# The set-up stage of a graph-attention kernel: row products three search pieces behind the copies they read, loads of W and x four pieces later

## The chip, the cores and the metric

The kernel runs on one core of a Trainium2 chip. The metric is device time in microseconds (us), of which less is better. The core has a tensor engine (TensorE, PE in the profile), a vector engine (VectorE, DVE), a scalar engine (ScalarE, ACT), GpSimd (POOL) and SyncE (SP), each with its own queue of instructions. ScalarE, SyncE and GpSimd also issue transfers (DMAs), which 16 DMA engines carry out.

## The reference

There are 4096 nodes with 128 features each, and a random 4096 x 4096 adjacency matrix of 0 and 1 in which a row has about 32 ones. Layer 0 is graph attention with 8 heads, layer 1 takes quantiles over a part of each node's neighbours. Cut to what matters:

```python
# layer 0
Wh = jnp.einsum('nd,hde->hne', nodes, W)
f1 = jnp.einsum('hnd,hd->hn', Wh, a1)
f2 = jnp.einsum('hnd,hd->hn', Wh, a2)
e = jax.nn.leaky_relu(f1[:, :, None] + f2[:, None, :], negative_slope=ALPHA)
att = jax.nn.softmax(jnp.where(mask, e, -9e15), axis=-1)
h = jax.nn.elu(jnp.einsum('hnm,hmd->hnd', att, Wh))
x = jax.nn.elu(cat @ W1 + b1)          # cat: the heads side by side
out = _layernorm(nodes + x, gamma, beta)
# layer 1: of each node's neighbours, without each skip-th, three quantiles
svals = jnp.sort(jnp.where(keep[:, :, None], x[None, :, :], big), axis=1)
agg = sum(w_q * picked(q) for q in (0.25, 0.5, 0.75))
agg = 0.5 * agg + 0.5 * x
out = agg @ W.T + b + x
```

The part that the change is in computes f1 and f2. The kernel does it as nodes times (W a1) and nodes times (W a2): 16 numbers for a node.

## The kernel before

The nodes are worked on in 32 tiles of 128, in three blocks of 4, 9 and 19 tiles. For a block the kernel first searches the adjacency rows for the neighbours' numbers (`neighbours`), then ranks the nodes by their number of neighbours, scatters one record for each node to DRAM, and then gathers the neighbours' feature rows from DRAM with indirect transfers and computes the attention. The search of the next block runs beside the attention of the one before. Layer 1 follows when all tiles are done: gathers, then sorting networks on VectorE.

The stage that matters here is the first: the search of the block of 4 tiles, with nothing to run beside it but the set-up. All of it stands ahead of the first gather. The order on TensorE, VectorE, ScalarE and GpSimd is fixed when the program is built, and in this stage it is the one in which the code names the instructions, except that at its end the small operations of the ranking stand among those that complete the records. An instruction that waits holds up whatever stands behind it on its engine. SyncE's queue is not ordered by the code in this way.

The search is a generator that stops after every piece. One piece (there are 43 for this block) handles 512 columns of one tile of 128 rows. TensorE makes a key for each column with two matmuls (L683, L686) from the signs of the adjacency row; there are two buffers for keys. VectorE takes the eight largest keys of each 128 columns (the "eights", four MAX8 at L650) one piece later. Beside that, for the tile before, it finds the next eight neighbours of the whole row (`best`: MAX8 at L655 and a replacement at L657). Pieces 0 to 31 make keys, pieces 8 to 39 find the best, and pieces 40 to 42 complete the records (L723 to L758). ScalarE turns an adjacency half-tile (128 x 2048, 1 MB) into signs (L644), once in four pieces and four pieces ahead of use; there are two buffers for signs. Right after each sign it issues the load of a later half-tile (L637); there are three buffers for those.

The set-up of the rows is a second generator, `node_rows` (L544), which is advanced by one step after every piece but the first (L326 to L328). It loads W (L550), a1, a2 (L554) and Wl (L556), then x in four quarters (L561), all from ScalarE's queue. VectorE multiplies W with a1 and a2 and sums (`wprod`, L567, L570), which gives `wa`. Then, for four tiles at a time, TensorE transposes x (L587), ScalarE copies the transposes to `xT` (L589), TensorE multiplies them with `wa` to `f_ps` (L581), and ScalarE copies that to `F` (L576). When all 32 tiles are done, VectorE clamps F into the records (L592) and SyncE stores x and f2 to `xt_d` (L594), from which the attention gathers. VectorE also computes a check on F (`sq` and `fm`, L604 to L609), and TensorE transposes Wl (L612).

After that VectorE, in `rank_by_count`, makes the ranks (L817 to L826), GpSimd scatters the records (L230), SyncE reads them back in the new order (L862, L888), and the first gather (L221) follows.

Of the kernel before, what the change touches and what calls it, by code (L numbers as in the profile page):

```python
# [9 lines left out]
F32 = mybir.dt.float32  # L10
# [9 lines left out]
P = 128  # L20
# [3 lines left out]
NT = N // P  # L24
# [220 lines left out]
def kernel(  # L245
# [61 lines left out]
    with tc.tile_pool(name="setup", bufs=1) as sp, tc.tile_pool(  # L307
# [15 lines left out]
        )  # L323
        iota(nc, rowi, [[1, P]])
        rows = node_rows(tc, sp, pp, rec, x, W, W_sb, a1, a2, Wl, wa, WlT, ident, bad, xt_d)
        for i, _ in enumerate(search(0, BLOCKS[0])):  # L326
            if i > 0:
# [216 lines left out]
def node_rows(tc, sp, pp, rec, x, W, W_sb, a1, a2, Wl, wa, WlT, ident, bad, xt_d):  # L544


    nc = tc.nc
    c = NT // 4
    load = nc.scalar.dma_start
    load(W_sb, W.rearrange("h d e -> d h e"))  # L550
    yield
    a_b = sp.tile([P, 2, H * D], F32, name="a_b")
    for i, a in enumerate((a1, a2)):
        load(a_b[:, i, :], a.rearrange("h d -> (h d)").partition_broadcast(P))  # L554
    wl_sb = sp.tile([P, D], F32, name="wl_sb")
    load(wl_sb, Wl)  # L556
    yield
    for i in range(4):
        for _ in range(3):
            yield  # L560
        load(  # L561
            rec[:, ts(i, c), R_X : R_X + D],
            x[ts(i, c * P), :].rearrange("(t p) d -> p t d", p=P),
        )
    for i in range(2):
        wprod = sp.tile([P, H, D], F32, name="wprod")
        nc.vector.tensor_tensor(  # L567
            wprod, W_sb, a_b[:, i, :].rearrange("p (h d) -> p h d", h=H), ALU.mult
        )
        nc.vector.tensor_reduce(wa[:, ts(i, H)], wprod, AX.X, ALU.add)  # L570
        yield
    F = sp.tile([P, NT, 2 * H], F32, name="F")
    xT = f_ps = None
    for t in range(0, NT + 8, 4):
        if f_ps is not None:
            nc.scalar.copy(F[:, t - 8 : t - 4, :], f_ps)  # L576
            f_ps = None
        if xT is not None:
            f_ps = pp.tile([P, 4, 2 * H], F32, name="f_ps")
            for u in range(4):  # L580
                nc.tensor.matmul(f_ps[:, u, :], lhsT=xT[:, ts(u, P)], rhs=wa, start=True, stop=True)  # L581
            xT = None
        yield
        if t < NT:
            xt_ps = pp.tile([P, 4 * P], F32, name="xt_ps")
            for u in range(4):
                nc.tensor.transpose(xt_ps[:, ts(u, P)], rec[:, t + u, R_X : R_X + D], ident)  # L587
            xT = sp.tile([P, 4 * P], F32, name="xT", bufs=2)
            nc.scalar.copy(xT, xt_ps)  # L589
        yield  # L590
    for dst, src in ((R_F1, F[:, :, 0:H]), (R_X + D, F[:, :, H:])):
        nc.vector.tensor_scalar(rec[:, :, dst : dst + H], src, FMAX, -FMAX, ALU.min, ALU.max)  # L592
    for i in range(4):
        nc.sync.dma_start(  # L594
            xt_d[ts(i, c * P), :].rearrange("(t p) w -> p t w", p=P),
            rec[:, ts(i, c), R_X:],
        )
    pad = sp.tile([P, XW], F32, name="pad")
    nc.gpsimd.memset(pad[:, 0:D], 0.0)
    nc.gpsimd.memset(pad[:, D:], PADF)  # L600
    nc.sync.dma_start(xt_d[N:, :], pad)
    yield
    sq = sp.tile([P, NT, 2 * H], F32, name="sq")
    nc.vector.tensor_tensor(sq, F, F, ALU.mult)  # L604
    fm = sp.tile([P, NT], F32, name="fm")
    nc.vector.tensor_reduce(fm, sq, AX.X, ALU.max)

    nc.vector.tensor_scalar(fm, fm, FMAX * FMAX, None, ALU.is_le)
    nc.vector.tensor_scalar(bad[:, 3, :], fm, -1.0, 1.0, ALU.mult, ALU.add)  # L609
    yield  # L610
    wl_ps = pp.tile([P, 4 * P], F32, name="xt_ps")[:, 0:D]
    nc.tensor.transpose(wl_ps, wl_sb, ident)  # L612
    nc.scalar.copy(WlT, wl_ps)
# [882 lines left out]
```

## Time and profile before

| | |
|---|---|
| median of three runs | 3682.77 us (3679.86 to 3687.81) |
| the profiled execution | 4612.32 us, of which its span is 4610.5 us |
| busy over the span: PE, DVE, ACT, POOL | 1260.0, 2754.3, 399.4, 2364.5 us |
| L826, the ranks are ready | at 94.81 us |
| L221, the first gather is issued | at 112.40 us |
| gathers for the attention (L221) | 1127, mean 967 ns |
| gathers for the quantiles (L221) | 1024, mean 1052 ns |

The profile is of one execution, which took about 930 us longer than the timed runs. Its page shows busy times of each engine, the clock that TensorE was granted in 40 equal slices of the span (115 us each), the costliest groups of instructions by line, and the transfers. A line of the timeline has the start in us, the duration in us, the engine, the line in the code, the operation, what it writes and reads, and in brackets how long the engine had been idle before and what ended that. A "q" behind an engine's name is its queue of transfer issues: the time given is that of the issue, not that of the transfer.

### The profile page before, as it was taken

Reading aid. Unit: us, or ns where it says so; the run is one execution under the profiler, and the core shown is the slowest. Engines: PE = TensorE matmul, PEld = TensorE weight load, DVE = VectorE, ACT = ScalarE, POOL = GpSimd, SP = SyncE. Lnnn points to the kernel's source line nnn. Section 1 sums busy time; section 2 is a strip of 40 time slices with the busy share of each in tenths; the row PEclk is TensorE's granted clock in tenths of the full one; section 3 lists DMA queues with packets and bytes.
Section 4 is the critical chain, followed back from the end, with each engine's and each line's share of the span. In section 5 each row is a group of like instructions: output and inputs, shape, how many; then the busy total and the mean of one; then the engine's idle time right before and its main releaser. Section 6 shows DMA issues by size and latency. Waiting matters only on the chain. (4 is left out here: it accounts for less than half of the span.)

```text
span 4610.5 us, 23017 instructions
## 1 busy us (share of the span) xinstructions
PE 1260.0 (27%) x5372; PEld 961.7 (21%) x5375; DVE 2754.3 (60%) x7608; ACT 399.4 (9%) x555; POOL 2364.5 (51%) x2344
## 2 busy tenths in 40 slices
PE   5264546555243425334245000000000000000001
PEld 2023323333243425324245000000000000000001
DVE  6274446655142212212254289989987977887788
ACT  2020212211011001000001000000000000000000
POOL 1616543243755566464532756677665355565530
PEclk9995556555556555555555555555555555555555
DMA  5321423220211111111110111111111011111100
GB/s 186 92 90 48 141 69 101 96 94 23 61 43 38 43 43 50 36 45 45 45 29 20 50 35 39 41 44 42 41 38 34 24 32 31 36 39 37 36 22 4
DMA packets 109537, 237.71 MB, mean 52 GB/s; under 512 B 47072, under 2 KB 63456, under 8 KB 101200
## 3 DMA queue, kind: packets, MB, share of 16 engines
q0 software_dynamic: 74464, 156.55, 12.2%
q10 hardware_dynamic: 14848, 70.85, 4.5%
q1 hardware_dynamic: 20080, 8.77, 0.8%
q8 instruction: 44, 0.72, 0.1%
q14 instruction: 101, 0.83, 0.1%
HBM read 224.85 MB, written 11.15 MB: 51 GB/s over the span
## 5 line engine op out<-in xcount | busy, mean ns | idle before, releaser
L221 POOL DMA_INDIRECT G<-xt_d,idx x1127 | 1090.3, 967 | 1109.5 <-PE y L1012 696.0
L221 POOL DMA_INDIRECT vals<-x_d,idx x1024 | 1076.9, 1052 | 337.5 <-issue 302.0
L1223 DVE TENSOR_TENSOR work<-work 128x512 f32<-128x512 f32 (+6 forms) x1405 | 960.6, 712 | 35.8 <-remote 22.1
L1223 DVE TENSOR_TENSOR work<-work,work 128x512 f32<-128x512 f32 (+5 forms) x958 | 605.6, 656 | 47.6 <-remote 35.7
L1242 PE MATMUL st_ps<-dg,goal 128*128 128x128 f32 x286 | 71.8, 430 | 1935.4 <-DVE goal L1223 1791.8
L1012 PE MATMUL y<-wide,G 128*128 128x32 f32 (+2 forms) x2254 | 463.1, 381 | 97.3 <-issue 71.6
L1242 PEld LDWEIGHTS st_ps<-dg,goal 128*128 128x128 f32 x286 | 63.9, 325 | 1941.5 <-issue 1940.6
L1012 PEld LDWEIGHTS y<-wide,G 128*128 128x128 f32 x2254 | 443.6, 297 | 120.4 <-issue 86.1
L976 DVE TENSOR_SCALAR rden<-small 4x256 f32<-4x256 f32 x32 | 13.0, 407 | 648.1 <-remote 583.6
L650 DVE MAX8 first<-key 128x8 f32<-128x128 f32 x1024 | 225.5, 282 | 253.6 <-remote 128.7
L230 POOL DMA_INDIRECT out_dram<-o,own_i x32 | 50.8, 1588 | 556.6 <-ACT o L1268 539.2
L1194 DVE COPY junk<-still 128x1 f32<-128x1 f32 x1295 | 194.6, 150 | 206.2 <-remote 97.4
L683 PE MATMUL key<-sgn,markb 128*128 128x512 bf16 x256 | 147.2, 575 | 398.9 <-DVE first L650 171.2
L982 PE MATMUL rz<-rden,ownT 4*128 4x32 f32 (+6 forms) x460 | 113.3, 416 | 515.9 <-DVE rden L977 431.4
L982 PEld LDWEIGHTS rz<-rden,ownT 4*128 4x128 f32 x460 | 101.8, 317 | 532.2 <-issue 364.0
L1031 PE MATMUL hT<-late,W_sb 128*128 128x128 f32 x512 | 112.8, 409 | 238.1 <-issue 160.2
L644 ACT ACTIVATE sgn<-adj_t 128x2048 bf16<-128x2048 int32 x64 | 122.1, 1908 | 557.3 <-PE key L683 273.5
L1223 DVE TENSOR_TENSOR work<-vals 128x1024 f32<-128x1024 f32 (+8 forms) x140 | 138.7, 1007 | 32.7 <-DMA vals<-x_d,idx 32.4
L1031 PEld LDWEIGHTS hT<-late,W_sb 128*128 128x128 f32 x512 | 104.7, 312 | 249.7 <-issue 167.1
L1241 ACT ACTIVATE dg<-ident,wt 128x128 f32<-128x128 f32 x143 | 47.6, 394 | 1191.8 <-PE st_ps L1242 1191.5
L686 PE MATMUL key<-parts,oneb 64*128 64x512 bf16 x256 | 146.5, 572 | 4.8 <-issue 4.6
L1042 PE MATMUL small<-W_sb,late 128*128 128x128 f32 x512 | 120.3, 429 | 33.4 <-DVE late L1039 33.4
(184 smaller groups left out, 1743.0 us busy)
## 6 DMA issues: line engine op xcount, KB each, us to landing
adj_t<-in_adj_dram ACTq DMA_DIRECT2D x64, 1024.0 KB
G<-xt_d,idx POOLq DMA_INDIRECT x1127
vals<-x_d,idx POOLq DMA_INDIRECT x1024
R<-rec_d SPq DMA_DIRECT2D x128, 26.2 KB
xt_d<-rec SPq DMA_DIRECT2D x4, 544.0 KB
rec<-in_x_dram ACTq DMA_DIRECT2D x4, 512.0 KB
narrow<-rec_d SPq DMA_DIRECT2D x72, 5.2 KB
a_b<-in_L_gnn_a_dram ACTq DMA_DIRECT2D x2, 512.0 KB
```

What stands on the lines that cost most here:

```text
L221: nc.gpsimd.indirect_dma_start(out=dst, out_offset=None, in_=rows, in_offset=bass.IndirectOffsetOnAxis(ap=idx, axis=0),)
L644: nc.scalar.activation(sgn, adj_t, AF.Sign, accum_out=cnt[:, i : i + 1])
L650: nc.vector.max(first[:, ts(c0 // CW + c, 8)], key[:, ts(c, CW)])
L683: nc.tensor.matmul(key, lhsT=markb, rhs=sgn[:, ts(b, 512)], start=True, stop=False)
L686: nc.tensor.matmul(key, lhsT=oneb[0:64, :], rhs=parts[1][:, ts(r - 1, 512)] if r else parts[0], start=False, stop=True)
L982: nc.tensor.matmul(rz[:, layer[i] * H : (layer[i] + w - g0) * H], lhsT=ownT[w][:, r, :], rhs=rden.rearrange("p (g r h) -> p r g h", r=k // ...
L1012: nc.tensor.matmul(yf[:, ts(g, c)], lhsT=G[:, col + j - a, 0:D], rhs=pf[:, ts(j, c)], start=(i == 0 and g % (w // 2) == w // 2 - 1), stop= ...
L1031: nc.tensor.matmul(hT[:, ts(h, P)], lhsT=consts["W_sb"][:, h, :], rhs=yT[:, h, :], start=True, stop=True)
L1042: nc.tensor.matmul(o, lhsT=hv[:, h, :], rhs=consts["W1_sb"][:, h, :], start=(h == 0), stop=(h == H - 1))
L1194: nc.vector.tensor_copy(junk, late["still"])
L1223: nc.vector.tensor_tensor(slots_of(dst, (j, c, s, m), size), slots_of(a, (i, c, s, m), size), slots_of(b, (i + d, c, s, m), size), op,)
L1242: nc.tensor.matmul(st_ps[:, u, :], lhsT=goal[:, (j * k + u) * D : (j * k + u + 1) * D], rhs=dg, start=(j == 0), stop=False,)
```

## The change

The change leaves every operation as it is and moves steps of `node_rows` to other places in the row of pieces. One more buffer for `xT` (three in place of two) is the only addition.

- The load of W moves from the first step to the fifth, those of a1, a2 and Wl from the second to the seventh. The four quarters of x are then two pieces apart and not three, so the first comes four pieces later, the last one piece later. The multiplication to `wa` and the transposes come one piece later.
- The product of four tiles with `wa` was made one piece after their transposes and their copy; it is now made three pieces after. The copy to F was made two pieces after the product and still is.
- The clamps, the stores to `xt_d`, the check on F and the transpose of Wl come three pieces later: they now stand among the pieces that complete the records.

```diff
@@ -547,8 +547,11 @@
     nc = tc.nc
     c = NT // 4
     load = nc.scalar.dma_start
+    for _ in range(4):
+        yield
     load(W_sb, W.rearrange("h d e -> d h e"))
-    yield
+    for _ in range(2):
+        yield
     a_b = sp.tile([P, 2, H * D], F32, name="a_b")
     for i, a in enumerate((a1, a2)):
         load(a_b[:, i, :], a.rearrange("h d -> (h d)").partition_broadcast(P))
@@ -556,7 +559,7 @@
     load(wl_sb, Wl)
     yield
     for i in range(4):
-        for _ in range(3):
+        for _ in range(2):
             yield
         load(
             rec[:, ts(i, c), R_X : R_X + D],
@@ -570,23 +573,24 @@
         nc.vector.tensor_reduce(wa[:, ts(i, H)], wprod, AX.X, ALU.add)
         yield
     F = sp.tile([P, NT, 2 * H], F32, name="F")
-    xT = f_ps = None
-    for t in range(0, NT + 8, 4):
-        if f_ps is not None:
-            nc.scalar.copy(F[:, t - 8 : t - 4, :], f_ps)
-            f_ps = None
-        if xT is not None:
+    turned, made = [], []
+    for t in range(0, NT + 12, 4):
+        if t >= 12:
+            nc.scalar.copy(F[:, t - 12 : t - 8, :], made.pop(0))
+        if 8 <= t < NT + 8:
             f_ps = pp.tile([P, 4, 2 * H], F32, name="f_ps")
+            xT = turned.pop(0)
             for u in range(4):
                 nc.tensor.matmul(f_ps[:, u, :], lhsT=xT[:, ts(u, P)], rhs=wa, start=True, stop=True)
-            xT = None
+            made.append(f_ps)
         yield
         if t < NT:
             xt_ps = pp.tile([P, 4 * P], F32, name="xt_ps")
             for u in range(4):
                 nc.tensor.transpose(xt_ps[:, ts(u, P)], rec[:, t + u, R_X : R_X + D], ident)
-            xT = sp.tile([P, 4 * P], F32, name="xT", bufs=2)
+            xT = sp.tile([P, 4 * P], F32, name="xT", bufs=3)
             nc.scalar.copy(xT, xt_ps)
+            turned.append(xT)
         yield
     for dst, src in ((R_F1, F[:, :, 0:H]), (R_X + D, F[:, :, H:])):
         nc.vector.tensor_scalar(rec[:, :, dst : dst + H], src, FMAX, -FMAX, ALU.min, ALU.max)
```

## The prediction

> **What bounds the kernel now.** I read the page's span and slices first, then the two stages' busy times, then the timeline from the first instruction to the first gather, and last the order in which the two built programs put their instructions on each engine.
>
> ```profile
> span 4610.5 us, 23017 instructions
> PEclk9995556555556555555555555555555555555555
> ```
>
> The change touches only what runs before the first gather, one of the forty slices. The reader is to see that it can win or lose microseconds, not per cent. The handover to the rest is this (start, duration, engine, line, operation):
>
> ```profile
> 94.81 0.17 DVE L826 CAST ranks<-rank 128x4 int32<-128x4 f32 x1
> 95.86 1.12 POOL L230 DMA_INDIRECT rec_d<-rec,ranks  x1 [54.61 <-issue]
> ...
> 112.40 0.97 POOL L221 DMA_INDIRECT G<-xt_d,idx  x1 [4.98 <-issue]
> ```
>
> VectorE computes the ranks, GpSimd scatters the records 1 us later, SyncE reads them back, GpSimd gathers. So this stage ends when VectorE reaches L826, and VectorE's idle time before it is what can be won. Busy time by stage (PE, PEld, DVE, ACT, POOL, clock, DMA share, GB/s):
>
> ```profile
> 20.00:40.00 20.00, 11.23 (x20) 1.94 (x19) 15.48 (x59) 8.01 (x8) 0.00 (x0) 1.00 1.05 358
> 40.00:60.00 20.00, 17.52 (x57) 9.80 (x57) 15.99 (x65) 6.49 (x11) 0.83 (x3) 1.00 0.35 117
> 60.00:80.00 20.00, 19.27 (x70) 12.86 (x70) 14.82 (x61) 6.80 (x13) 0.00 (x0) 1.00 0.40 126
> ```
>
> From 20 to 40 us the DMA engines are full; from 40 to 80 us TensorE is. VectorE has two kinds of gap. The first:
>
> ```profile
> 16.60 0.33 ACTq L637 DMA_DIRECT2D adj_t<-in_adj_dram  x1
> 17.61 0.39 ACTq L550 DMA_DIRECT2D W_sb<-in_L_gnn_W_dram  x1
> 18.03 2.34 ACTq L554 DMA_DIRECT2D a_b<-in_L_gnn_a_dram  x2
> 20.41 0.54 ACTq L556 DMA_DIRECT2D wl_sb<-in_L_gnn_W_dram  x1
> 21.00 1.91 ACT L644 ACTIVATE sgn<-adj_t 128x2048 bf16<-128x2048 int32 x1 [9.77 <-DMA adj_t<-in_adj_dram]
> 23.05 0.58 PE L683 MATMUL key<-sgn,markb 128*128 128x512 bf16 x1 [5.10 <-ACT sgn L644]
> 24.21 0.89 DVE L650 MAX8 first<-key 128x8 f32<-128x128 f32 x4 [4.34 <-PE key L686]
> ```
>
> ScalarE's queue issues W, a1, a2 and Wl ahead of the third sign, and the sign starts right after the last issue. Its bracket blames a transfer, but the issues before it fill the time up to 20.95. Key 8 then comes late and VectorE loses 4.34 us. The second kind:
>
> ```profile
> 48.34 1.12 PE L587 MATMUL xt_ps<-ident,rec 128*128 128x128 f32 x4
> 49.26 0.63 PE L683 MATMUL key<-sgn,markb 128*128 128x512 bf16 x1
> 50.36 1.89 PE L581 MATMUL f_ps<-wa,xT 128*128 128x16 f32 x8
> 52.08 0.59 PE L683 MATMUL key<-sgn,markb 128*128 128x512 bf16 x1
> ```
>
> The next transposes start at 53.14, so two pieces cost TensorE 4.80 us: transposes 0.92, key 1.10, products 1.72, key 1.06. It does not wait: the products start exactly 0.54 after the key's second half, and the copy xT had ended at 50.08. VectorE needs only 3.2 for two pieces. Its gaps in 43 to 75 us, from the same timeline, are 0.41, 0.36, 1.14, 0.62, 0.90, 0.29, 1.07, 0.32, 1.10, 0.36, 1.14, 0.62: together 8.33 us.
>
> **What the Trainium skill says.** "TensorE: Matmul & The Clock Gate", section "Back-to-back issue gap", gives N/1.2 ns for a cold matmul, 427 ns for 512 columns, and "LDWEIGHTS" adds P/1.2, 107 ns: 0.53 us. The trace has 0.54, although its clock row reads 1.00 here. "What's actually happening" has the warm clock at twice that; no run here shows it yet. The same page, "Architectural detail", calls ACT and DVE strict FIFO: the sign held behind the issues agrees. "DMA: Bandwidth & Descriptors", "Issuing engines are not separate DMA queues", says that all queues share the same 16 DMA engines; the share of 1.05 agrees, so landing times must be counted over all queues. "Perfetto Trace Analysis", the part on HWDGE DMA instructions, warns that data movement lies outside a DMA instruction's window; so I estimate landings from bytes.
>
> **Part 1, loads later.** No instruction is added or removed. In the new program ScalarE's order is: adjacency load (16.60, as before), third sign, next adjacency load, and only then W, a1, a2, Wl. The third adjacency tile was asked for by 2.15 us. Up to 12 us 3.7 MB had moved (sum of two-us windows: 37, 255, 402, 423, 413, 337 GB/s), more than the three tiles and W1 together (3.67 MB), so it should be there. The sign starts at 16.98 and not at 21.00: 4.02 us earlier, and key 8 and VectorE with it (24.21 to 20.19; it is free at 19.86, so 0.33 us of gap stays). Bound from the other side: a2's issue at 18.9 waits for that tile's semaphore, so the tile is there by then at the latest, and the gain is at least 2.1. I take 4.0.
>
> What now stands behind: the fourth sign, behind an adjacency issue (0.33), W 0.39, a1 and a2 2.34 and Wl 0.54, starts at 22.75. Key 12 needs it 2.05 later, at 24.8; it would otherwise come at 28.49 - 4.02 = 24.47. VectorE is a full microsecond behind TensorE there, so 0.3 is hidden; every microsecond of slower issue beyond that would show.
>
> W and a1 are needed by wprod, now after piece 16: 20.19 plus seven pieces (9.5 us to the eights of key 14, 1.15 for that piece, 0.35, 1.8) gives 33.0. Landing, estimated: 5.6 MB had moved by 19.4; six adjacency tiles, W1, the vectors, fills, W, a1 and a2 are 8.9 MB; the rest, 3.3 MB at 360 GB/s (20 to 34 us), takes 9 us: 28.4. Slack 4.6 us. The first x quarter comes 1.6 MB later, 33, and is needed at 41.2. Both hidden; if the cover were gone, the whole lateness would be VectorE's.
>
> **Part 2, products later.** Before, the transposes follow pieces 18, 20, ... 32 and the products pieces 19, 21, ... 33. After, the transposes follow 19, 21, ... 33 and the products 22, 24, ... 36. The last key is number 31. So between key 18 and key 31 TensorE had seven transposes and six products; it now has six and five. The lag removes no wait, as TensorE had none; it moves work behind the last key, where TensorE is idle.
>
> In time: VectorE sets the pace up to key 18, its eights move from 44.78 to 40.76. Pieces 19 to 21 hold two transposes and no products, so VectorE goes on at 1.6 a piece; key 22 ends at 46.4. From there TensorE is the bound again: products 1.72, key to 49.2, then four periods of 4.79. Key 31 starts at 48.1 + 19.2 = 67.3, before at 73.22. Its eights come 1.2 later, at 68.5 against 74.42: 5.95 us earlier. So part 2 gives 5.95 - 4.02 = 1.9 of the 8.33; the rest stays.
>
> **Part 3, the tail.** VectorE has the same 77 instruction rows from these eights to L826, only the two clamps and the four operations on sq stand later. The clamps need F: after key 31 TensorE does transposes, products, transposes, two products (7.0 us, to 75.3), the last copy ends at 76.4. The clamps stand at 74.42 to 86.77 less 2.15 of moved operations, 10.2 after the eights: 78.7. Slack 2.3 us. SyncE's four stores of xt_d then start at 79.2, 2.2 earlier than before (81.41). Their 2.23 MB took 8 us and overlap an adjacency load by about a microsecond, so they land near 88 to 89, ahead of the first scatter (95.86 - 5.95 = 89.9), and the gather that needs them is at 106.4. Nothing is added on POOL. Behind this, the engines' orders are the same; the first gather waits also for TensorE's and ScalarE's use of the third xT buffer, which is over 30 us before.
>
> **Sum.** 4.0 + 1.9 = 5.9 us. The profiled execution, 4612.3 us with 1.8 outside its span, would take 4606.4. The runs' median, 3682.8, is 25% shorter than the profiled execution; the stage is early and I find no reason to scale, so 3676.9. A measurement of this kernel can tell about 0.2%, 7.4 us, from no change.
>
> **Rivals.**
> (B) All of VectorE's gaps go, 4.0 + 8.3: 3670.4. For it: the gaps are all named as waits for keys. Against: two pieces' TensorE work sums to the period, so waits for copies are not what fills it. 0.14.
> (C) In the runs without a profile TensorE is warm, halving its 4.8 us below VectorE's 3.2; the second kind of gap is not there to win, and 4.0 or less is left: 3678.8. For it: the runs are 25% shorter. Against: 0.54 a key all along in the trace. 0.18.
> (D) W and a1 land late. VectorE stands at wprod; the forecast is used up when they land after 33.0 + 5.9 = 38.9. Before, the DMA engines empty only at 43.6; if W landed then, the wait is 10.6 and the time 3682.8 - 5.9 + 10.6 = 3687.5. For it: full DMA engines, one more adjacency tile ahead. Against: the 4.6 us of slack. 0.08.
> (A) The forecast: 0.60.
>
> **How the numbers follow.** A spans 3674 to 3680 by the bounds of part 1 and the issue times. To hold 8 in 10 the range takes in C, most of B and a few us of run-to-run spread (the three runs lie 8 us apart): 3669 to 3684. Faster by over 0.2%: nearly all of B and 0.17 of A's 0.60 by spread, 0.30. Slower by over 0.2%: most of D and a little spread, 0.08. The rest, 0.62, is within.
>
> **What would show it.** Right: third sign near 17, before the W issue; no 4.3 us gap at piece 8; eights of key 31 near 68.5; L826 near 88.9; first gather near 106.4; period still 4.8 us in the middle. Wrong: a VectorE gap ahead of L570 (D), periods under 4 us (B), or a first gather moved by 6 us and a total that does not follow.

## The result, and the profile after

The changed kernel took 3683.1 us (median of 12 runs, 3667.4 to 3691.6). The kernel before, run beside it, took 3687.2 us (12 runs, 3679.9 to 3696.0). The ratio is 0.9983 with a 95% interval of 0.9969 to 0.9997: 6.3 us less, and between 1.1 and 11.4 (it is not the ratio of the two medians, which lie 4.1 us apart). That is on the edge of what a measurement of this kernel can tell, and within the 0.2% that the prediction called no change.

The page of the changed kernel begins with its span and, further down, the clock that TensorE was granted in 40 slices of the span:

```profile
span 3688.3 us, 23015 instructions
...
PEclk9975665565575555555555555555555555555555
```

The two profiled executions differ by 922 us, which is no effect of the change: the profile of before and all of the later experiments are of executions with longer waits behind the set-up, in which either kernel takes some 4550 to 4600 us (medians). The set-up stage can be compared all the same, because in it the same operations last as long in both: a half of a key (one of its two matmuls) has a pitch of 0.54 us in either, and the changed kernel reaches the ranks within 0.22 us of the profile shown here in two such longer executions. So what follows reads that stage alone.

Busy time by stage of the changed kernel (window, then PE, PEld, DVE, ACT, POOL in us, clock, DMA share, GB/s):

```profile
20.00:40.00 20.00, 11.72 (x21) 2.05 (x21) 19.07 (x70) 6.01 (x6) 0.83 (x3) 1.00 1.05 354
40.00:60.00 20.00, 19.44 (x62) 10.78 (x63) 16.22 (x73) 6.36 (x10) 0.00 (x0) 1.00 0.53 172
60.00:80.00 20.00, 15.86 (x63) 11.73 (x62) 16.15 (x74) 7.08 (x15) 0.00 (x0) 1.00 0.32 103
```

VectorE works 19.07 us of the first window, before 15.48. In all three it works 51.44 us, before 46.29. The difference, 5.15 us, is about how much earlier the stage's work is done. TensorE is busy to the last from 40 to 60 us, as it was before from 60 to 80: the same work stands earlier.

The timeline of the changed kernel (start, duration, engine, line, operation; the line numbers behind L550 are two to four higher than before):

```profile
16.90 0.33 ACTq L641 DMA_DIRECT2D adj_t<-in_adj_dram  x1
17.34 1.91 ACT L648 ACTIVATE sgn<-adj_t 128x2048 bf16<-128x2048 int32 x1 [6.20 <-PE key L690]
19.37 0.33 ACTq L641 DMA_DIRECT2D adj_t<-in_adj_dram  x1
19.73 0.46 ACTq L552 DMA_DIRECT2D W_sb<-in_L_gnn_W_dram  x1
20.22 1.41 ACTq L557 DMA_DIRECT2D a_b<-in_L_gnn_a_dram  x2
20.55 0.89 DVE L654 MAX8 first<-key 128x8 f32<-128x128 f32 x4 [0.69 <-PE key L690]
21.66 1.95 ACTq L559 DMA_DIRECT2D wl_sb<-in_L_gnn_W_dram  x1
23.66 1.91 ACT L648 ACTIVATE sgn<-adj_t 128x2048 bf16<-128x2048 int32 x1 [4.32 <-PE key L690]
...
33.17 1.22 DVE L570 TENSOR_TENSOR wprod<-W_sb,a_b 128x1024 f32<-128x1024 f32 x1
...
49.59 1.12 PE L590 MATMUL xt_ps<-ident,rec 128*128 128x128 f32 x4
50.50 0.63 PE L687 MATMUL key<-sgn,markb 128*128 128x512 bf16 x1
...
51.60 1.89 PE L584 MATMUL f_ps<-wa,xT 128*128 128x16 f32 x8
...
54.49 0.89 DVE L654 MAX8 first<-key 128x8 f32<-128x128 f32 x4 [1.06 <-PE key L690]
...
68.87 0.89 DVE L654 MAX8 first<-key 128x8 f32<-128x128 f32 x4 [1.39 <-PE key L690]
...
75.91 0.20 ACT L579 COPY F<-f_ps 128x64 f32<-128x64 f32 x1
...
79.31 0.49 DVE L596 TENSOR_SCALAR rec<-F 128x256 f32<-128x256 f32 x2
...
89.41 0.17 DVE L830 CAST ranks<-rank 128x4 int32<-128x4 f32 x1
90.45 1.12 POOL L230 DMA_INDIRECT rec_d<-rec,ranks  x1 [51.17 <-issue]
...
107.30 0.97 POOL L221 DMA_INDIRECT G<-xt_d,idx  x1 [5.15 <-issue]
```

Read from the top: the third sign follows its adjacency issue at 17.34, and W, a1, a2 and Wl are issued behind it. Key 8's eights wait 0.69 us where they waited 4.34. `wprod` has no bracket: W and a1 were there. In the middle the two pieces' pattern of TensorE is as before, with transposes every 4.79 us (49.59, then 54.38), and VectorE's brackets are again about 0.3 and 1.1. The eights of key 31 stand at 68.87. In the profile of before they stood here:

```profile
74.42 0.90 DVE L650 MAX8 first<-key 128x8 f32<-128x128 f32 x4 [0.62 <-PE key L686]
```

The last copy to F ends 3.2 us before the clamps, the ranks come 5.40 us earlier (94.81 to 89.41) and the first gather 5.10 (112.40 to 107.30).

### The profile page after: what moved, and what is told of

Read it like the earlier page. It is cut to its first block, busy times and chain, and to the rows that moved or that the text cites. A ratio compares the mean times of both kernels' runs of the same rounds, so it can differ in the third digit from the quotient of the medians.

```text
span 3688.3 us, 23015 instructions
## 1 busy us (share of the span) xinstructions
PE 1235.0 (33%) x5375; PEld 940.7 (26%) x5375; DVE 2743.8 (74%) x7608; ACT 397.5 (11%) x555; POOL 2365.6 (64%) x2344
## 5 line engine op out<-in xcount | busy, mean ns | idle before, releaser
L221 POOL DMA_INDIRECT G<-xt_d,idx x1127 | 1121.8, 995 | 500.7 <-issue 324.8
L221 POOL DMA_INDIRECT vals<-x_d,idx x1024 | 1052.4, 1028 | 336.4 <-issue 298.1
L1016 PE MATMUL y<-wide,G 128*128 128x32 f32 (+2 forms) x2254 | 447.5, 376 | 27.2 <-DVE wide L1003 27.2
L1016 PEld LDWEIGHTS y<-wide,G 128*128 128x128 f32 x2254 | 427.0, 289 | 51.6 <-DVE wide L1003 30.2
L955 DVE TENSOR_TENSOR z<-G,f1x 128x128 f32<-128x128 f32 (+5 forms) x93 | 29.4, 328 | 430.8 <-DMA G<-xt_d,idx 429.5
L970 PE MATMUL small<-z,own 128*4 128x32 f32 (+6 forms) x460 | 50.1, 274 | 343.8 <-ACT z L962 343.8
```

What stands on the lines that cost most here:

```text
L221: nc.gpsimd.indirect_dma_start(out=dst, out_offset=None, in_=rows, in_offset=bass.IndirectOffsetOnAxis(ap=idx, axis=0),)
L1016: nc.tensor.matmul(yf[:, ts(g, c)], lhsT=G[:, col + j - a, 0:D], rhs=pf[:, ts(j, c)], start=(i == 0 and g % (w // 2) == w // 2 - 1), stop= ...
```

## The experiments

The theory: the two parts act one after the other on VectorE's chain, the loads with some 4 us and the lag of the products with some 2, and what the ranks gain goes whole into the time. The main rivals: only one of the parts does anything; or a gain so early is lost later. The first four kernels ran together, the next four together, the last two together.

| | third sign | wait at key 8 | eights of key 31 | ranks | key 8's eights to ranks | first gather | ratio to before, 95% interval |
|---|---|---|---|---|---|---|---|
| before, its profile | 21.00 | 4.34 | 74.42 | 94.81 | 70.60 | 112.40 | |
| before_again | 19.99 | 3.35 | 73.41 | 93.79 | 70.59 | 112.08 | 0.9989, 0.9963 to 1.0016 |
| loads_only | 17.28 | 0.64 | 70.59 | 91.10 | 70.60 | 108.64 | 0.9957, 0.9929 to 0.9985 |
| lag_only | 20.70 | 4.05 | 72.64 | 93.16 | 69.25 | 111.16 | 1.0003, 0.9975 to 1.0031 |
| delay40 | 17.86 | 1.23 | 69.39 | 130.07 | 108.99 | 147.90 | 1.0071, 1.0042 to 1.0099 |
| after, its profile | 17.34 | 0.69 | 68.87 | 89.41 | 68.86 | 107.30 | 0.9983, 0.9969 to 0.9997 |
| after_again | 17.07 | 0.43 | 68.63 | 89.19 | 68.90 | 107.04 | 0.9962, 0.9941 to 0.9983 |
| after_third | 17.09 | 0.45 | 68.63 | 89.19 | 68.88 | 107.24 | 1.0011, 0.9974 to 1.0048 |
| w_after_x | 17.27 | 0.61 | 75.13 | 95.68 | 75.20 | 113.53 | one run, 4596.6 us |
| late6 | 17.86 | 1.21 | 64.59 | 85.76 | 64.69 | 103.56 | 0.9977, 0.9944 to 1.0010 |
| late6_again | 17.27 | 0.62 | 65.08 | 86.25 | 65.77 | 104.01 | 1.0007, 0.9981 to 1.0032 |
| late7 | 16.70 | none | 61.82 | 84.76 | 64.85 | 104.52 | 0.9989, 0.9963 to 1.0015 |

All times are microseconds. The sixth column counts from the start of key 8's eights: what happens ahead of key 8, where the issues hold up the third sign, drops out of it. The kernel before took 4559.8, 4597.4 and 4558.2 us in the three groups. Its repeat in the same group came out at 0.9989, 5 us away from itself and with 12 us of interval to each side, so the total cannot part effects of 2 and 4 us here; the milestones in the traces can.

### before_again: the kernel before, unchanged

> The kernel before, unchanged, beside itself. It shows how far two equal kernels lie apart, and where the first gather stands in a second execution. Theory (the set-up stage alone decides): ratio 1.000 within 0.0015, ranks ready (L826) at 94.8 us, first gather at 112.4, two pieces of TensorE's dense part in 4.8 us. Rival (TensorE runs at twice the clock in undisturbed runs, so the second kind of gap isn't there): a key matmul to the next in 0.27 us and not 0.54, and the ranks earlier than 90.

In its timeline the same issues stand ahead of the third sign:

```profile
17.38 0.39 ACTq L550 DMA_DIRECT2D W_sb<-in_L_gnn_W_dram  x1
17.80 1.62 ACTq L554 DMA_DIRECT2D a_b<-in_L_gnn_a_dram  x2
...
19.46 0.48 ACTq L556 DMA_DIRECT2D wl_sb<-in_L_gnn_W_dram  x1
19.99 1.91 ACT L644 ACTIVATE sgn<-adj_t 128x2048 bf16<-128x2048 int32 x1 [8.95 <-issue]
...
23.20 0.89 DVE L650 MAX8 first<-key 128x8 f32<-128x128 f32 x4 [3.35 <-PE key L686]
```

The issues of a1 and a2 took 1.62 us, in the first profile 2.34, the issue of Wl 0.48 instead of 0.54, and the sign came 1.01 us earlier. The bracket now reads "issue", where the first profile named the adjacency transfer. So the sign waited for the issues ahead of it on ScalarE's queue, not for its data. It also gives the spread of one kernel's set-up: 1.0 us in the ranks, 0.3 at the first gather, where the fourth scatter happened to wait longer. All of that 1.0 us arises ahead of key 8: from its eights to the ranks it is 70.59 us here and 70.60 in the first profile.

### loads_only: the loads later, the products where they were

```diff
-    turned, made = [], []
-    for t in range(0, NT + 12, 4):
+    xT = f_ps = None
+    for t in range(0, NT + 8, 4):
...
-            xT = sp.tile([P, 4 * P], F32, name="xT", bufs=3)
+            xT = sp.tile([P, 4 * P], F32, name="xT", bufs=2)
```

(the loop of the kernel before, the loads of the changed one)

> The loads of W, a1, a2, Wl and x as in the changed kernel, the products one piece behind their transposes as before. Theory: the third sign starts near 17.3, the 4.3 us gap shrinks to 0.7, so 3.7 us come from here; TensorE then has six products between key 18 and key 31 and not five: eights of key 31 near 70.4 (before 74.4, changed 68.9), ranks ready near 91.0 (before 94.8, changed 89.4), ratio 0.9990. Rival (the gain is one of both parts together, or of the lag alone): ranks no earlier than 93.

```profile
70.59 0.89 DVE L653 MAX8 first<-key 128x8 f32<-128x128 f32 x4 [1.39 <-PE key L689]
...
91.10 0.17 DVE L829 CAST ranks<-rank 128x4 int32<-128x4 f32 x1
...
108.64 0.98 POOL L221 DMA_INDIRECT G<-xt_d,idx  x1 [4.99 <-issue]
```

The ranks come 3.71 us earlier than in the profile of before, 2.69 earlier than in before_again. Key 8 comes earlier by the same 3.71, and from there to the ranks it is 70.60 us as before. This is the larger part of the change, and it acts without the other. The total came out 20 us (7 to 32) below the kernel before, where 0.9990, some 5 us, was expected; nothing in the set-up accounts for the rest.

### lag_only: the products later, the loads where they were

```diff
-    for _ in range(4):
-        yield
     load(W_sb, W.rearrange("h d e -> d h e"))
-    for _ in range(2):
-        yield
+    yield
...
-        for _ in range(2):
+        for _ in range(3):
             yield
```

> The products three pieces behind, the loads as before. Theory: the 4.3 us gap stays; five products and not six between the keys 18 and 31: eights of key 31 near 73.0, ranks ready near 93.4, ratio 0.9996. Rival (TensorE's products did wait for ScalarE's copies, and the lag takes all of these waits away): VectorE's gaps between 43 and 75 us go from 8.3 to under 3, ranks before 89.

```profile
65.84 0.89 DVE L651 MAX8 first<-key 128x8 f32<-128x128 f32 x4 [1.11 <-PE key L687]
67.85 0.89 DVE L651 MAX8 first<-key 128x8 f32<-128x128 f32 x4 [0.36 <-PE key L687]
70.63 0.89 DVE L651 MAX8 first<-key 128x8 f32<-128x128 f32 x4 [1.14 <-PE key L687]
72.64 0.89 DVE L651 MAX8 first<-key 128x8 f32<-128x128 f32 x4 [0.62 <-PE key L687]
...
93.16 0.17 DVE L827 CAST ranks<-rank 128x4 int32<-128x4 f32 x1
```

The ranks come 1.65 us earlier than in the profile of before. The wait at key 8 is still 4.05, and VectorE's last eight brackets before key 31 (0.91, 0.29, 1.07, 0.33, 1.11, 0.36, 1.14, 0.62) are those that the prediction lists for before, to 0.01 us. If the lag had removed a wait of TensorE's, its periods would be shorter and these brackets smaller. There are only fewer of them, ten and not twelve: one transpose group and one product group have gone behind the last key.

The parts seem to add up, 3.71 + 1.65 = 5.36 against 5.40 together, but so close a sum is in part luck. Of the 1.65, 0.30 comes from key 8, which was earlier here because the row of issues ahead of the third sign happened to start earlier (17.31 against 17.61). Counted from key 8, the lag gives 1.35 us alone (69.25 against 70.60) and 1.74 beside the early loads (68.86 against 70.60 in loads_only). The parts add up to within 0.4 us; where these 0.4 come from was not looked into.

### delay40: the changed kernel with 32 multiplications on VectorE before the ranks

```diff
         for _ in rows:
             pass
+        spare = sp.tile([P, H * D], F32, name="spare")
+        for _ in range(32):
+            nc.vector.tensor_tensor(
+                spare,
+                W_sb.rearrange("p h d -> p (h d)"),
+                W_sb.rearrange("p h d -> p (h d)"),
+                ALU.mult,
+            )
```

> The changed kernel with 32 more multiplications of 128x1024 on VectorE ahead of the ranks, 1.25 us each, 40 us in all; their result isn't used. It asks whether a time won or lost ahead of the first gather reaches the end whole. Theory: everything behind the first gather keeps its distances, so ranks ready near 129.4 and the total 40 us (36 to 44) over the changed kernel, 34 over the one before: ratio 1.0092. Rival (part is taken up later, where GpSimd or VectorE waits anyway): under 30 us over the changed kernel, ratio under 1.0065.

The ranks come 40.7 us later than in the changed kernel, the first gather 40.6 later and 35.5 later than in the kernel before. The time went up by 0.71%, 32 us, with an interval of 19 to 45 (of the 4560 us that the kernel before took here). That a delay of the set-up is wholly taken up behind it is thereby excluded. That all of it arrives is near the middle of the interval; that only half of it does (19 of 35.5) is its lower end, so the rival, a ratio under 1.0065, is not excluded. The prediction's scale of 1 fits, and is not shown more closely than that; that a gain arrives as a delay does is assumed.

### after_again and after_third: the changed kernel, unchanged

> The changed kernel, unchanged, timed once more beside the one before. Theory: ranks ready (L826 of the kernel before, here L830) at 89.4 us, first gather at 107.3, each within 0.6 us, and a ratio of 0.998 to 0.999 (6 us less). Rival (the gain is one of the other executions' spread): ratio 1.000 and the ranks anywhere between 89 and 95.

> The changed kernel once more, as the mark for late6_again. Theory: first gather near 107.3 us, time some 5 us below the kernel before and 4 above late6_again. Rival: all three the same within their intervals.

The set-up repeats: the ranks at 89.19 both times, 0.22 us from the profile. The totals do not: 17 us less than before (8 to 27) in one group, 5 more in the other (12 less to 22 more). Those two intervals hardly meet, so on executions of this length something of ten microseconds or more moves between groups of runs that is not in the set-up. The three measurements together say that the change does no harm that can be seen; the size of its gain rests on the traces and on the first comparison.

### w_after_x: W, a1, a2 and Wl behind all four quarters of x

```diff
     for _ in range(4):
         yield
+    for i in range(4):
+        quarter(i)
+        yield
     load(W_sb, W.rearrange("h d e -> d h e"))
...
-        load(
-            rec[:, ts(i, c), R_X : R_X + D],
...
```

> The changed kernel with the loads in another order: the four quarters of x at steps 5 to 8, W at step 9, a1, a2 and Wl at step 11, so 2.1 MB of x and one more adjacency half-tile stand ahead of W and a1. It asks whether landings follow from the bytes ahead, and what a late one costs. Theory: 5.6 MB had moved by 19.4 us and 12.1 MB have to for a1, at 360 GB/s, so it lands near 37.3; VectorE reaches the multiplication with W at 33.2 and waits 4 us; the ranks come that much later, near 93.5. Rival (the loads have much more slack than the bytes say): no wait there, ranks at 89.4.

```profile
19.30 0.33 ACTq L644 DMA_DIRECT2D adj_t<-in_adj_dram  x1
19.66 6.96 ACTq L551 DMA_DIRECT2D rec<-in_x_dram  x3
26.68 1.91 ACT L651 ACTIVATE sgn<-adj_t 128x2048 bf16<-128x2048 int32 x1 [7.40 <-issue]
...
29.89 0.89 DVE L657 MAX8 first<-key 128x8 f32<-128x128 f32 x4 [2.89 <-PE key L693]
...
30.52 4.36 ACTq L566 DMA_DIRECT2D a_b<-in_L_gnn_a_dram  x2
...
39.41 1.23 DVE L573 TENSOR_TENSOR wprod<-W_sb,a_b 128x1024 f32<-128x1024 f32 x1 [3.24 <-DMA a_b<-in_L_gnn_a_dram]
```

Here the load that VectorE's `wprod` reads is late, by 3.24 us, and that wait is seen at once ahead of L573. But there is a second one that the landing estimate does not contain: three issues of x held ScalarE's queue for 6.96 us, the fourth sign stood behind them, and key 12's eights waited 2.89. Together 6.13 of the 6.27 us by which the ranks are later than in the changed kernel. The wait at `wprod` was forecast at 4 us, with a1 landing near 37.3; the bracket ends at 39.41, so the landing estimate was 2.1 us too early. The wait came out near the forecast only because VectorE reached `wprod` 3 us late as well, and the ranks, forecast at 93.5, came at 95.68. So how late a load may be issued is bounded twice, by its landing and by the time its issue takes from the instructions behind it.

### late6 and late7: more of the products behind the last key

The changed kernel makes three of the eight product groups behind key 31. These make six and seven; late6 has five `xT` buffers, late7 eight. The clamps stand one piece further behind in late6, four in late7.

```diff
-        if 8 <= t < NT + 8:
+    at = [5, 9, 13, 14, 15, 16, 17, 18]     # late6
+    at = [7, 14, 15, 16, 17, 18, 19, 20]    # late7
+    for k in range(max(at) + 2):
...
+        if k in at:
             f_ps = pp.tile([P, 4, 2 * H], F32, name="f_ps")
...
+        if k % 2 == 1 and k < 16:
             xt_ps = pp.tile([P, 4 * P], F32, name="xt_ps")
```

(k counts the pieces from 18, so k = 13 is the piece of the last key)

> The changed kernel with two products among the keys and six behind the last one (five and three), five buffers for xT, the clamps three small operations later. Theory (TensorE's work between the keys is what holds VectorE up, each product 1.7 us): eights of key 31 near 64.4 us (changed 68.9), TensorE done with the products near 76, just ahead of the ranking's first matmul; ranks ready near 85.0, first gather near 102.9, ratio to the kernel before 0.9975. Rival (the products behind the last key hold up the ranking or the stores as much as they free): ranks at 88 or later.

> One product among the keys, seven behind the last one, eight buffers for xT, the clamps and the stores to xt_d at the very end, ahead of the ranks. Theory: eights of key 31 near 62.7 us; TensorE ends the products near 76.4, one microsecond after the ranking's first matmul is wanted, so the ranks near 84.2; the stores run beside the scatters and land near 93, ahead of the first gather near 102, ratio 0.9972. Rival (the stores, now beside the scatters, slow these, or the first gather waits for them): first gather at 105 or later.

Late6, its timeline: the only waits of over 0.3 us for keys from 42 us on, then the ranking's first wait, the clamps and their stores, the ranks and the gather.

```profile
52.29 0.89 DVE L659 MAX8 first<-key 128x8 f32<-128x128 f32 x4 [1.12 <-PE key L695]
...
60.17 0.89 DVE L659 MAX8 first<-key 128x8 f32<-128x128 f32 x4 [1.37 <-PE key L695]
...
76.53 0.22 DVE L805 COPY low<-key 128x63 f32<-128x63 f32 x1 [0.61 <-PE key L802]
...
78.91 4.07 SPq L603 DMA_DIRECT2D xt_d<-rec  x4
...
85.76 0.17 DVE L835 CAST ranks<-rank 128x4 int32<-128x4 f32 x1
...
103.56 0.97 POOL L221 DMA_INDIRECT G<-xt_d,idx  x1 [5.16 <-issue]
```

Late7, the same view:

```profile
75.40 0.22 DVE L805 COPY low<-key 128x63 f32<-128x63 f32 x1 [2.25 <-PE key L802]
...
80.77 4.06 SPq L603 DMA_DIRECT2D xt_d<-rec  x4
...
84.76 0.17 DVE L835 CAST ranks<-rank 128x4 int32<-128x4 f32 x1
85.81 1.12 POOL L230 DMA_INDIRECT rec_d<-rec,ranks  x1 [47.15 <-issue]
90.76 0.96 POOL L230 DMA_INDIRECT rec_d<-rec,ranks  x1 [3.83 <-DMA rec_d<-rec,ranks]
93.42 0.96 POOL L230 DMA_INDIRECT rec_d<-rec,ranks  x1 [1.70 <-DMA rec_d<-rec,ranks]
```

In late6 three product groups of 1.72 us fewer stand between the keys, 5.2 us of TensorE's work. The eights of key 31 come 4.28 us earlier than in the changed kernel (64.59). Key 8 was 0.52 us later here, so counted from it the gain is 4.80. It is less than 5.2, since VectorE is now the bound for most of the way: only two waits for keys are left, one at each product group. The ranking's first wait takes 0.61 back; the ranks come 3.65 earlier, the gather 3.74. That TensorE's work, and not a wait for a copy, sets the pace in the middle is thus shown by taking work away.

Late7 shows where this ends. The eights of key 31 come another 2.77 us earlier (61.82), of which 1.16 is an earlier key 8 and 1.61 the seventh product. But the products now stand before the ranking's first matmul, and VectorE waits 2.25 us for it, where in late6 it waited 0.61. That takes all of the gain: counted from key 8, the ranks come after 64.85 us, in late6 after 64.69. And the stores of x, issued at 80.77, are still moving when the first scatter goes out: the DMA engines carry 282 to 294 GB/s from 82 to 88 us, 261 from 88 to 90, and nothing from 90 to 92. The second scatter waits 3.83 us for the first instead of 1.7 to 1.9 as in all other runs, and the gather comes later than in late6 though the ranks were 1.00 us earlier: at 104.52, between the 102 that was expected and the rival's 105. That the stores cause the long scatter is inferred from the overlap; the stores were not taken away by themselves.

Late6 was measured once more:

> The kernel late6 once more, beside the changed kernel on the same chip. Theory (the set-up's microseconds carry whole): first gather near 103.6 us, 3.7 before the changed kernel's 107.3, and the time some 9 us below the kernel before. Rival (the gain of the early stage is lost to later waits): time as the kernel before, interval about 1.

```profile
20.21 2.88 ACTq L557 DMA_DIRECT2D a_b<-in_L_gnn_a_dram  x2
...
24.76 1.91 ACT L653 ACTIVATE sgn<-adj_t 128x2048 bf16<-128x2048 int32 x1 [5.49 <-PE key L695]
...
27.97 0.89 DVE L659 MAX8 first<-key 128x8 f32<-128x128 f32 x4 [0.98 <-PE key L695]
```

Its gather was at 104.01, 3.2 us before that of after_third beside it. Here the issues ahead of the fourth sign took longer than in the changed kernel's profile, the sign came at 24.76 instead of 23.66, and key 12's eights waited 0.98 us. The loads stand in the same order in both kernels, so this can happen to the changed kernel too.

In the total late6 took 3 us more than the kernel before (9 less to 15 more), where 9 less was expected. The intervals of late6 and of the changed kernel in that group both include no change, and they overlap. A version that is earlier in the set-up is there; that it takes less time is not shown.

## Why the prediction was right, and where its sizes were off

**The total.** 5.9 us less was forecast, from the profiled time of before; measured were 6.3 (1.1 to 11.4) in time, and 5.1 at the first gather. That 6.3 lies so near 5.9 is luck, given an interval of ten microseconds; what confirms the forecast is the stage's own times. The forecast of 3676.9 stands on the median of the first three runs; the median of all twelve of the kernel before lies 4.4 us higher. The result is 6.2 us above the forecast, near the upper end of the stated range of 3669 to 3684, and by itself would not tell the forecast from rival C (3678.8).

**Part 1, loads later: right, 0.3 us too large.** The sign was forecast at 16.98 and came at 17.34. The term that was mis-sized is the start of the adjacency issue, taken "as before" at 16.60. It was 16.90 (0.06 us more were lost behind it), and over the twelve executions of all kernels it lies between 16.27 (late7) and 17.43 (delay40); what it waits for was not found. With it the gap at key 8 is 0.69 and not 0.33. The gain of 4.0 is 3.7 in loads_only. It was also measured against one execution of before in which the issues were long; against before_again it would be 2.7.

**What stands behind the sign: right, with the room nearly used up.** The fourth sign was forecast at 22.75 and came at 23.66. Of the 0.91, 0.36 is the later third sign and most of the rest the issues of a1, a2 and Wl, which took 3.36 us together and not 2.88. The prediction let a key 12 that is 0.3 us late hide behind the microsecond by which VectorE was behind TensorE. With the third sign where it was, key 12 would have come at 24.83 and started at 25.71, so 0.9 us of that microsecond were used. VectorE still shows no wait, but late6_again, with the same loads and a sign 1.10 us later still, waited 0.98. So in the changed kernel the hold on ScalarE's queue is just hidden, by an issue time that varies from run to run; w_after_x shows a larger one.

**Landing of W and a1: right, but not tested by the changed kernel.** `wprod` started at 33.17 without a wait, forecast 33.0. The landing itself cannot be read from that. Where it can be read, in w_after_x, the same way of estimating was 2.1 us too early, less than the 4.6 us of slack that the prediction had left.

**Part 2, products later: right.** "The lag removes no wait" and "it moves work behind the last key" are both what lag_only shows. Key 31 was forecast at 67.3 and came at 67.71, its eights 68.5 and 68.87. The difference is the 0.36 of part 1. VectorE's waits from 43 us on sum to 6.52 (0.84, 1.06, 0.31, 1.09, 0.34, 1.12, 0.37, 1.39), before 8.33: 1.81 less, forecast 1.9. "TensorE had none" holds for the stretch up to key 31; behind it the products of before did wait once for a copy, 0.73 us at 77.87, without holding up the clamps.

**Part 3, the tail: right.** Clamps 79.31 (78.7), stores 79.82 (79.2), ranks 89.41 (88.9), gather 107.30 (106.4). The steps behind the ranks took 17.89 us, before 17.59. The 0.3 lies among the transfers there, which vary as much in a kernel that is the same: 17.85 in after_again, 18.05 in after_third, 18.29 in before_again.

**The rivals.** B (all gaps go) is out: the brackets of 1.1 us are still there, and late6 shows that removing most of them takes more products moved behind the last key. C (TensorE at twice the pace in the short executions) is out: the profiled execution of the changed kernel is itself a short one, 3690.1 us in a spread of 3667.4 to 3691.6, and its keys still have a pitch of 0.54 us. "TensorE: Matmul & The Clock Gate", section "What's actually happening", of the Trainium skill, gives a warm TensorE twice the clock of a cold one, after some 3.4 us of sustained work. Here TensorE was busy for 19.44 of the 20 us from 40 to 60 us and kept the pitch it had at the start; the measurement decides, and in this stage neither kind of execution shows the faster pace. D (W and a1 late) did not occur; w_after_x produced it.

## What to carry to other kernels

A load that is issued from an engine's queue costs that engine the time of the issue, so issue first what feeds the engine's own next instruction, and look at what stands behind the issue and not only at when the data land. Where an engine is the bound through a stretch and idles right behind it, moving its work past the end of the stretch is worth at most the moved work, until the other engine becomes the bound; it ends where the work meets the first instruction of the next stage. An effect of a few microseconds early in a long kernel is better read from milestones in two traces, repeated once for their spread, than from the total; and counted from a point behind the source of that spread (here key 8), the two profiles of before agreed to 0.01 us and the three of the changed kernel to 0.04.

## What was not expected of the hardware

The time of a DMA's issue varied by a factor of nearly nine for loads of the same size. In the changed kernel the first quarter of x took 0.45 us on ScalarE's queue at 26.07, the last 3.98 us at 33.77; in w_after_x three of them took 6.96 us. Full DMA engines alone do not explain it, since their share was 1.01 from 26 to 27 us and 1.10 from 33.7 to 37.8. It fits a queue that holds the issuer back while many transfers stand before it, but the runs do not show that mechanism itself. The issues of a1 and a2, two instructions, took from 1.10 us (late6) to 2.88 (late6_again, the same kernel). A wait for a scatter grew from about 1.7 to 3.83 us in the one run (late7) in which stores moved beside it for another four microseconds.
